# Value projection by rows, carried to the windows through DRAM, in a window-attention and mixture-of-experts kernel

## The chip, the cores and the metric

The kernel runs on one core of a Trainium2 chip. A core has a matmul engine (TensorE, "PE" in the profile, its weight loads "PEld"), VectorE ("DVE"), ScalarE ("ACT"), GpSimd ("POOL") and SyncE ("SP"), which here only issues DMA transfers. The metric is the device time of one execution in microseconds (us), as the median of several runs; less is better.

## The reference

The input `x` is (2, 128, 256, 256) in float32. It goes through a normalisation over channels, a window attention with a residual, a second normalisation and a mixture of eight experts with a residual.

```
x = x + conv(ln_c(x))                 # window attention
t = tokens(x)
t = t + ffn(ln_t(t))                  # top 2 of 8 experts

conv: qkv = W_qkv · x;  queries from 8 x 8 windows,
      keys and values from 12 x 12 windows around them (padding 2, outside the image 0)
      attn = softmax(q·k * scale + relative position + fixed mask)
      out  = W_out · (attn · v)       # 4 heads of 32 channels
ffn:  p = softmax(t · router_w + b);  the two largest, made to sum to 1
      out = sum over the two of p_e * (t · expert_w[e] + expert_b[e])
```

The fixed mask leaves, of each 12 x 12 window, only every second row and column that has the parity of the query's own. So the image falls into four planes (row parity by column parity) that do not meet in the attention; in each, a window has 4 x 4 queries and 6 x 6 keys.

## The kernel before

The image is cut into strips of eight rows, 32 for each of the two images. A strip has four planes of 4 x 128 positions. The main loop (from L779) goes over all 256 planes; one iteration does the attention of plane n, the projections of plane n + 1 (`project`), the normalisation and routing of rows (`norms`, `route`), and the experts of a quarter of an earlier strip (`Experts`). The order of instructions on every engine in this loop is the order of the program text (`manual_schedule`), so an engine that waits holds up everything written after it.

Two windows side by side share their keys and values in a run of 10 columns by 6 rows, 60 positions in a slot of 64. A plane has 16 such pairs; two pairs at a time fill 128 partitions (`HP` is 8). `xn` holds the normalised input of a strip with channels in the partitions, by plane, row (six: one row above, four, one below, `KR`) and column. `place` says at which of the six places of a window a row stands; the places turn from strip to strip, so that four rows are new in a strip and two stay.

The values need the positions in the partitions. Before the change, `columns` (L326) lets POOL copy the windows' columns from `xn` into `xcol`, overlaps included. Then `project` multiplies each of the eight column blocks of 128 with the weights `wv` (`values`, L366): four products into a PSUM tile `pvv` at the start of the projections, four more at their end, each group copied to `vv` by ACT (L376). `attend` (L477) uses `vv` as the weights of its products (L496).

The other steps that the prediction speaks of, in their order within an iteration:

- TensorE: the scores of plane n (L448, then L465), values and `pu` (L384), `pk` (L396), `pq` (L418), four expert products (L686), the attention (sums L486, values L496), the row sums `plt` (L554), the other values, three expert products, `po` (L524), one expert product. A float32 product is two passes, each a weight load and a matmul.
- DVE: routing (L587 to L619), `gT` (L625), the transpose `uT` of `pu` (L386), `au` (L349, L354), `xs` (L671) and six products `xe` (L677), the end of the experts (L692), the transposes and the division of the attention (L506 to L516), `plg` (L563), `rstd` (L228 to L235, with ACT for the logarithm and the exponential in L232 and L233), the residual `xt` (L529).
- POOL: a marker copy `last` (L681) that holds POOL back until DVE has made its six products, the two other products `xe` (L677), `ln1` (L272) between them, the halo copy (L246) in every fourth plane, and the columns of plane n + 2 (L331).
- SP: two `gd` transfers (L633), `rb` (L637, a row that `ln1` waits for), `sb` (L666), eight `gb` (L661), a load `xt` (L115), a store (L722). Before a `gb` fetch, ACT or DVE touches the tile, which holds the transfer back until then.

PSUM tiles named by `mm_tile` share three buffers in rotation: a tile gets the buffer of the one three before it and waits until that one has been read.

From n = 6 on, `addr_align` (L793) fills TensorE's instructions up so that every iteration begins at the same slot of a block of 256, in which instructions are fetched; `FIRST_LIMIT` instructions of the iteration lie in its first block.

Of the kernel before, what the change touches and what calls it, by code (L numbers as in the profile page):

```python
# [17 lines left out]
P = 128  # L18
# [25 lines left out]
KR, KC = 6, 10  # L44
NK = KR * KC
SLOT = 64
BLOCK, FIRST_LIMIT = 256, 95
NU = 9


# [1 line left out]
def kernel(  # L52
# [42 lines left out]
    def ctile(shape, name):  # L95
        return const.tile(shape, F32, tag=name, name=name)
# [101 lines left out]
    xn, xcol, kcol = [], [], []  # L198
    for i in range(2):
        xn.append(ctile([P, 2, 2, KR, PC + 2], f"xn{i}"))  # L200
        nc.gpsimd.memset(xn[i][:, :, :, :, 0 : PC + 2 : PC + 1], 0.0)
    for i in range(4):
        xcol.append(ctile([P, HP, 2, SLOT], f"xcol{i}"))
        kcol.append(ctile([P, NP, SLOT], f"kcol{i}"))
        nc.gpsimd.memset(xcol[i][:, :, :, NK:], 0.0)
        nc.gpsimd.memset(kcol[i][:, :, NK:], 0.0)
        nc.gpsimd.memset(kcol[i][:, 0, 0:NK:KC], 0.0)
        nc.gpsimd.memset(kcol[i][:, NP - 1, KC - 1 : NK : KC], 0.0)
# [9 lines left out]
    def rstd(p4, k0, k1, name):  # L218

        u, r = (
            small.tile([P, 2, NT], F32, tag=v, name=f"{v}_{name}")[:, k0:k1] for v in ("u", "r")
        )
        mean, sq = (
            p4[:, :, E + 2 * k0 + j : E + 2 * k1 : 2].rearrange("p t k -> p k t") for j in range(2)
        )
        nc.vector.tensor_copy(r, mean)  # L228
        nc.vector.tensor_tensor(u, r, r, ALU.mult)
        nc.vector.scalar_tensor_tensor(u, u, -1.0, sq, ALU.mult, ALU.add)  # L230
        nc.vector.scalar_tensor_tensor(u, u, 0.0, epsc[:, k0:k1], ALU.max, ALU.add)
# [23 lines left out]
    def runs(i, rows):  # L255

        out = []
        for k in rows:
            if out and place(i, k) == out[-1][1] + out[-1][2]:
                out[-1][2] += 1  # L260
            else:
                out.append([k, place(i, k), 1])
        return out
# [59 lines left out]
            ln1(i, k, pb, nc.vector)  # L323
        yield

    def columns(n):  # L326

        i, pl = divmod(n, 4)
        for k, at, m in runs(i, ln_rows(i)):
            for half in range(2):  # L330
                nc.gpsimd.tensor_copy(  # L331
                    xcol[pl][:, :, half, at * KC : (at + m) * KC].rearrange(
                        "p t (r c) -> p t r c", c=KC
                    ),
                    windows(xn[i % 2][:, pl // 2, pl % 2, k : k + m], half * HP, HP),
                )
        for k, s in ((0, 0), (KR - 1, NS - 1)):
            if strips[i][1] == s:
                c0 = place(i, k) * KC
                nc.gpsimd.memset(xcol[pl][:, :, :, c0 : c0 + KC], 0.0)  # L340
                nc.gpsimd.memset(kcol[pl][:, :, c0 : c0 + KC], 0.0)

    def shift(uT, n, state):

# [12 lines left out]
    def project(n, state):  # L357

        i, pl = divmod(n, 4)
        xp = xn[i % 2][:, pl // 2, pl % 2]  # L360
        inner = xp[:, 1 : 1 + PR, 1 : PC + 1]
        xl, kk = xcol[pl], kcol[pl]

        vv = work.tile([P, HP, P], F32, tag="vv", name=f"vv{n}")

        def values(t0):  # L366
            pv = mm_tile(f"pvv{n}_{t0}")
            for t in range(4):
                nc.tensor.matmul(  # L369
                    pv[:, t * P : (t + 1) * P],  # L370
                    lhsT=xl[:, t0 + t].rearrange("p a k -> p (a k)"),
                    rhs=wv,
                    start=True,
                    stop=True,
                )
            nc.scalar.copy(vv[:, t0 : t0 + 4, :].rearrange("p t c -> p (t c)"), pv)  # L376

        values(0)
        yield

        pu = mm_tile(f"pu{n}")
        nc.tensor.matmul(pu, lhsT=wrel, rhs=inner, start=True, stop=True)  # L384
        uT = work.tile([P, PR, 4, 32], F32, tag="uT", name=f"uT{n}", bufs=1)
        nc.vector.transpose(uT, pu.rearrange("p (a m s) -> p a s m", a=PR, s=4))  # L386
# [28 lines left out]
        yield  # L415

        pq = mm_tile(f"pq{n}")
        nc.tensor.matmul(pq, lhsT=wq, rhs=inner, start=True, stop=True)  # L418
        qs = work.tile([P, 2 * NP, PR, 4], F32, tag="qs", name=f"qs{n}")
        nc.scalar.copy(  # L420
            qs.rearrange("p m a s -> p a m s"), pq.rearrange("p (a m s) -> p a m s", a=PR, s=4)
        )
        yield

        values(4)
        state.update(qs=qs, kk=kk, vv=vv)
        yield

    def windows(rows, n0, count):
# [315 lines left out]
            next(part)  # L745
    if len(strips) > 1:
        halo(1)
    columns(0)
    states = {0: {}}
    for _ in project(0, states[0]):  # L750
        pass
    states[0]["shift"]()
    if n_planes > 1:
        columns(1)

# [22 lines left out]
    with tc.manual_schedule(engines={ET.PE, ET.DVE, ET.Activation, ET.Pool, ET.SP}):  # L778
        for n in range(n_planes + 7):  # L779
# [32 lines left out]
            next(ahead, None)  # L812
            if n + 1 < n_planes:
                states[n + 1]["shift"]()
            next(ahead, None)
            next(ahead, None)
            for e in (4, 6, 7, 5):
# [26 lines left out]
            new.fetch(3, dve)  # L844
            while to_store:
                store(*to_store.pop())
            next(ahead, None)
            ex.product(0)
            made = next(norm, None)
# [76 lines left out]
```

The softmax here doesn't subtract the row's maximum and nothing guards it: scores larger than these inputs give would overflow.

## Time and profile before

| what | us |
| --- | --- |
| median of three runs | 4484.65 |
| lowest and highest run | 4484.2 and 4484.88 |
| span of the profiled execution, first to last instruction | 4480.1 |
| PE busy | 4422.6 |
| DVE busy | 3996.2 |
| ACT busy | 1467.7 |
| POOL busy | 1317.7 |

For the profiled execution the profile gives the span; the 4.55 us between it and the median of the runs are what lies around it. The mean granted clock of TensorE is 0.997. In the 40 equal slices of the span every engine's share is the same from the second slice to the last but one, so one plane of the loop stands for all. A line of the groups names the source line, engine, operation, output and inputs, shapes and count, then the busy time and the mean of one (ns), and after the bar the engine's idle time ahead of it with what ended that. A line of the timeline gives the start, the length, the engine, the line and the tiles. A line of the waits says who waited for whom, for how long in all, how often, and the longest. A line of the windows gives a stretch, its length and the busy time of each engine (PE, PEld, DVE, ACT, POOL) with the number of instructions, then the granted clock, the share of the DMA engines and GB/s.

### The profile page before, as it was taken

Reading aid. Unit: us, or ns where it says so; the run is one execution under the profiler, and the core shown is the slowest. Engines: PE = TensorE matmul, PEld = TensorE weight load, DVE = VectorE, ACT = ScalarE, POOL = GpSimd, SP = SyncE. Lnnn points to the kernel's source line nnn. Section 1 sums busy time; section 2 is a strip of 40 time slices with the busy share of each in tenths; the row PEclk is TensorE's granted clock in tenths of the full one; section 3 lists DMA queues with packets and bytes.
Section 4 is the critical chain, followed back from the end, with each engine's and each line's share of the span. In section 5 each row is a group of like instructions: output and inputs, shape, how many; then the busy total and the mean of one; then the engine's idle time right before and its main releaser. Section 6 shows DMA issues by size and latency. Waiting matters only on the chain. (4 is left out here: it accounts for less than half of the span.)

```text
span 4480.1 us, 224632 instructions
## 1 busy us (share of the span) xinstructions
PE 4422.6 (99%) x96321; PEld 2683.3 (60%) x96321; DVE 3996.2 (89%) x11850; ACT 1467.7 (33%) x4022; POOL 1317.7 (29%) x1815
## 2 busy tenths in 40 slices
PE   7999999999999999999999999999999999999997
PEld 5666666666666666666666666666666666666653
DVE  5899999999899999998989999999999999989887
ACT  3333333333333333333333333333333333333321
POOL 1232323232323233232323232323232323232321
PEclk9999999999999999999999999999999999999999
DMA  2565666566656666666666566666665666566655
GB/s 83 174 191 185 192 185 192 186 191 185 193 184 192 185 191 187 189 188 188 189 187 189 187 190 185 193 183 193 184 193 185 192 185 192 186 191 186 190 164 186
DMA packets 519284, 828.12 MB, mean 185 GB/s; under 512 B 124186, under 2 KB 125850, under 8 KB 518298
## 3 DMA queue, kind: packets, MB, share of 16 engines
q1 hardware_dynamic: 517568, 813.46, 58.3%
q8 instruction: 769, 12.60, 1.1%
q14 instruction: 217, 1.78, 0.2%
q10 hardware_dynamic: 730, 0.29, 0.0%
HBM read 737.95 MB, written 75.56 MB: 182 GB/s over the span
## 5 line engine op out<-in xcount | busy, mean ns | idle before, releaser
L686 PE MATMUL acc<-xe,ew 128*128 128x512 f32 x4096 | 1889.0, 594 | 19.6 <-DVE gb L660 18.8
L686 PEld LDWEIGHTS acc<-xe,ew 128*128 128x128 f32 x4096 | 758.8, 190 | 885.7 <-issue 861.8
L677 DVE TENSOR_TENSOR xe<-xs,gb 128x512 f32<-128x512 f32 x1536 | 950.9, 687 | 10.2 <-PE acc L686 0.7
L681 POOL COPY last<-xe 128x1 f32<-128x1 f32 x256 | 47.9, 187 | 3060.8 <-DVE gb L660 3054.6
L376 ACT COPY vv<-pvv 128x512 f32<-128x512 f32 x512 | 299.8, 586 | 1395.7 <-PE pvv L369 1379.6
L677 POOL TENSOR_TENSOR xe<-xs,gb 128x512 f32<-128x512 f32 x512 | 650.8, 1272 | 5.9 <-PE att L496 2.5
L369 PE MATMUL pvv<-wt,xcol 128*128 128x128 f32 x4096 | 594.3, 288 | 2.5 <-POOL xcol L331 1.5
L369 PEld LDWEIGHTS pvv<-wt,xcol 128*128 128x128 f32 x4096 | 496.4, 191 | 64.8 <-issue 51.8
L272 POOL TENSOR_TENSOR xn<-xt,rb 128x512 f32<-128x512 f32 x249 | 375.0, 1506 | 66.5 <-DMA rb<-gd 55.9
L465 PE MATMUL att<-qs,kcol 32*64 32x32 f32 x32768 | 392.4, 226 | 0.8 <-issue 0.7
L465 PEld LDWEIGHTS att<-qs,kcol 32*64 32x64 f32 x32768 | 391.0, 130 | 1.0 <-issue 1.0
L496 PEld LDWEIGHTS att<-pT,vv 64*32 64x32 f32 x32768 | 348.0, 105 | 39.4 <-issue 2.5
L496 PE MATMUL att<-pT,vv 64*32 64x32 f32 x32768 | 343.2, 200 | 2.3 <-issue 2.3
L473 ACT ACTIVATE pT<-att 128x1024 f32<-128x1024 f32 x256 | 261.9, 1023 | 243.1 <-PE att L465 239.7
L548 ACT ACTIVATE sq<-xt 128x512 f32<-128x512 f32 x505 | 292.7, 631 | 0.0
L354 DVE STREAM_TRANSPOSE au<-auT 128x512 f32<-128x512 f32 x256 | 269.2, 1052 | 9.0
L524 PE MATMUL po<-o,wt 128*128 128x512 f32 x512 | 262.0, 593 | 6.1 <-DVE o L516 3.2
L384 PE MATMUL pu<-xn,wrel 128*128 128x512 f32 x512 | 262.5, 594 | 0.0
L407 ACT COPY kcol<-pk 128x560 f32<-128x560 f32 (+2 forms) x344 | 174.1, 506 | 268.2 <-PE pk L396 265.3
L418 PE MATMUL pq<-xn,wt 128*128 128x512 f32 x512 | 262.0, 593 | 0.0
L396 PE MATMUL pk<-xn,wt 128*128 128x512 f32 (+2 forms) x528 | 261.0, 578 | 0.0
L386 DVE STREAM_TRANSPOSE uT<-pu 128x512 f32<-128x512 f32 x256 | 182.8, 714 | 78.0 <-PE pu L384 77.0
(2697 smaller groups left out, 5243.8 us busy)
## 6 DMA issues: line engine op xcount, KB each, us to landing
gb<-gd SPq DMA_DIRECT2D x2048, 256.0 KB, 4.0
xt<-in_x_dram SPq DMA_DIRECT2D x256, 256.0 KB, 4.9
sb<-gd SPq DMA_DIRECT2D x256, 256.0 KB, 3.5
out_dram<-xt SPq DMA_DIRECT2D x256, 256.0 KB, 4.2
rb<-gd SPq DMA_DIRECT2D x249, 256.0 KB, 3.3
gd<-gT SPq DMA_DIRECT2D x516, 16.0 KB, 3.0
ew<-in_L_ffn_expert_w_dram SPq DMA_DIRECT2D x1, 512.0 KB, 5.0
eb<-in_L_ffn_expert_b_dram SPq DMA_DIRECT2D x1, 512.0 KB, 5.7
```

What stands on the lines that cost most here:

```text
L272: eng.tensor_tensor(xn[i % 2][:, :, :, k, 1 : PC + 1], ln1_src(i, k).rearrange("p (y j x) -> p y x j", y=2, x=2), rb.rearrange("p (y j x) ...
L354: nc.vector.transpose(au.rearrange("p m a s -> p a s m"), auT[n % 2])
L369: nc.tensor.matmul(pv[:, t * P : (t + 1) * P], lhsT=xl[:, t0 + t].rearrange("p a k -> p (a k)"), rhs=wv, start=True, stop=True,)
L376: nc.scalar.copy(vv[:, t0 : t0 + 4, :].rearrange("p t c -> p (t c)"), pv)
L384: nc.tensor.matmul(pu, lhsT=wrel, rhs=inner, start=True, stop=True)
L418: nc.tensor.matmul(pq, lhsT=wq, rhs=inner, start=True, stop=True)
L465: nc.tensor.matmul(sc[rows, h, 32 * t : 32 * t + 32], lhsT=kk[hp, half * HP + t, :], rhs=qs[hp, m0 : m0 + 2].rearrange("p m a s -> p (m a ...
L496: nc.tensor.matmul(av[hp, half, 32 * t : 32 * t + 32], lhsT=vv[rows, t, hp], rhs=pT[rows, h, 32 * t : 32 * t + 32], start=True, stop=True,)
L524: nc.tensor.matmul(po, lhsT=wo, rhs=state["o"].rearrange("p f z -> p (f z)"), start=True, stop=True)
L548: nc.scalar.activation(sq, src, AF.Square)
L677: eng.tensor_tensor(self.xe[e], self.xs, self.gb.pop(e), ALU.mult)
L686: nc.tensor.matmul(self.acc, lhsT=ew[:, e, :], rhs=self.xe.pop(e), start=(e == 0), stop=not self.xe)
```

## The change

`columns` and `xcol` go. Each row of a strip's plane that is new is projected once: its 128 positions are the columns of one product with `wv`, four rows into one PSUM tile `pv` (five rows in an image's first strip, three in its last), and ACT copies the tile to `vr` (`value_rows`). `pu` stands ahead of these products. SP writes `vr` into a DRAM tile `vrows` by place and position (`send_values`, after the `uT` and `au` steps), and later in the same iteration, after the store, reads it back into the windows `vwin` (`take_values`): one transfer for each new row and each half of the pairs, over ten partitions with eight pieces of 512 bytes. `vwin` has the layout that `vv` had, and keeps the two rows that stay. The border columns of `vrows` are zeroed once; `borders` zeroes the rows outside the image.

In `rstd`, the square of the mean takes one factor from PSUM (`mean`) and no longer both from the copy `r`. `FIRST_LIMIT` goes from 95 to 99.

```diff
-BLOCK, FIRST_LIMIT = 256, 95
+BLOCK, FIRST_LIMIT = 256, 99
...
+    zero = ctile([P, 2, P], "zero")
+    nc.gpsimd.memset(zero, 0.0)
...
-        xcol.append(ctile([P, HP, 2, SLOT], f"xcol{i}"))
+        vwin.append(ctile([P, HP, P], f"vwin{i}"))
-        nc.gpsimd.memset(xcol[i][:, :, :, NK:], 0.0)
+        vrows.append(dram.tile([KR, PC + 2, P], F32, tag=f"vrows{i}", name=f"vrows{i}", bufs=1))
+        nc.gpsimd.memset(vwin[i], 0.0)
+        nc.sync.dma_start(vrows[i][:, 0 : PC + 2 : PC + 1, :], zero[0:KR])
...
-        nc.vector.tensor_tensor(u, r, r, ALU.mult)
+        nc.vector.tensor_tensor(u, r, mean, ALU.mult)
...
+    def value_rows(n):
+        i, pl = divmod(n, 4)
+        xp = xn[i % 2][:, pl // 2, pl % 2]
+        rows, sent = list(ln_rows(i)), []
+        for part in (rows[-4:], rows[:-4]):
+            if not part:
+                continue
+            pv = mm_tile(f"pv{n}_{part[0]}")
+            m = len(part)
+            for j, k in enumerate(part):
+                nc.tensor.matmul(pv[:, j * P : (j + 1) * P],
+                    lhsT=xp[:, k, 1 : PC + 1], rhs=wv, start=True, stop=True)
+            vr = work.tile([P, 4, P], F32, tag="vr", name=f"vr{n}_{part[0]}")
+            nc.scalar.copy(vr[:, 0:m].rearrange("p r c -> p (r c)"), pv[:, : m * P])
+            sent.append((part, vr))
+        return sent
+    def send_values(n, sent):
+        i, pl = divmod(n, 4)
+        for part, vr in sent:
+            for k, at, m in runs(i, part):
+                nc.sync.dma_start(
+                    vrows[pl][at : at + m, 1 : PC + 1, :].rearrange("r c d -> c r d"),
+                    vr[:, k - part[0] : k - part[0] + m])
+    def take_values(n):
+        i, pl = divmod(n, 4)
+        s = strips[i][1]
+        for k in range(0 if s == 0 else 2, KR):
+            at = place(i, k)
+            for half in range(2):
+                p0 = half * SLOT + at * KC
+                src = vrows[pl][at, half * HP * 8 : half * HP * 8 + KC, :].unsqueeze(1)
+                dims = [list(d) for d in src.ap]
+                dims[1] = [8 * P, HP]
+                nc.sync.dma_start(vwin[pl][p0 : p0 + KC],
+                                  bass.AP(src.tensor, src.offset, dims))
...
-        values(0)
-        yield
         pu = mm_tile(f"pu{n}")
         nc.tensor.matmul(pu, lhsT=wrel, rhs=inner, start=True, stop=True)
+        state["sent"] = value_rows(n)
+        yield
...
-        values(4)
-        state.update(qs=qs, kk=kk, vv=vv)
+        state.update(qs=qs, kk=kk, vv=vwin[pl])
...
                 states[n + 1]["shift"]()
+                send_values(n + 1, states[n + 1]["sent"])
...
                 store(*to_store.pop())
+            if n + 1 < n_planes:
+                take_values(n + 1)
...
-                columns(n + 2)
+                borders(n + 2)
```

More of the change, by code (lines that the diff above doesn't have):

```diff
@@ L196 @@
     nc.vector.tensor_copy(wrel, pr[:, :P])
-    xn, xcol, kcol = [], [], []
+    xn, vwin, vrows, kcol = [], [], [], []
+    zero = ctile([P, 2, P], "zero")
+    nc.gpsimd.memset(zero, 0.0)
     for i in range(2):
@@ L324, in first_norms, with borders @@
         yield
-    def columns(n):
+    def borders(n):
         i, pl = divmod(n, 4)
[L329 to L336, printed above, removed]
         for k, s in ((0, 0), (KR - 1, NS - 1)):
@@ L338, in columns @@
             if strips[i][1] == s:
-                c0 = place(i, k) * KC
-                nc.gpsimd.memset(xcol[pl][:, :, :, c0 : c0 + KC], 0.0)
-                nc.gpsimd.memset(kcol[pl][:, :, c0 : c0 + KC], 0.0)
+                at = place(i, k)
+                nc.gpsimd.memset(kcol[pl][:, :, at * KC : (at + 1) * KC], 0.0)
+                nc.sync.dma_start(vrows[pl][at, 1 : PC + 1, :], zero[:, 0, :])
+    def value_rows(n):
[8 more added lines that the diff above has]
+            for j, k in enumerate(part):
+                nc.tensor.matmul(
+                    pv[:, j * P : (j + 1) * P],
+                    lhsT=xp[:, k, 1 : PC + 1],
+                    rhs=wv,
+                    start=True,
+                    stop=True,
+                )
+            vr = work.tile([P, 4, P], F32, tag="vr", name=f"vr{n}_{part[0]}")
+            nc.scalar.copy(
+                vr[:, 0:m].rearrange("p r c -> p (r c)"), pv[:, : m * P]
+            )
+            sent.append((part, vr))
+        return sent
@@ new lines, in send_values @@
+    def send_values(n, sent):
[4 more added lines that the diff above has]
+                    vrows[pl][at : at + m, 1 : PC + 1, :].rearrange("r c d -> c r d"),
+                    vr[:, k - part[0] : k - part[0] + m],
+                )
+    def take_values(n):
+        i, pl = divmod(n, 4)
+        s = strips[i][1]
+        for k in range(0 if s == 0 else 2, KR):
+            at = place(i, k)
+            for half in range(2):
[3 more added lines that the diff above has]
+                dims[1] = [8 * P, HP]
+                nc.sync.dma_start(
+                    vwin[pl][p0 : p0 + KC], bass.AP(src.tensor, src.offset, dims)
+                )
@@ L361, in project @@
         inner = xp[:, 1 : 1 + PR, 1 : PC + 1]
[L362 to L376, printed above, removed]
-        values(0)
-        yield
+        kk = kcol[pl]
         pu = mm_tile(f"pu{n}")
         nc.tensor.matmul(pu, lhsT=wrel, rhs=inner, start=True, stop=True)
+        state["sent"] = value_rows(n)
+        yield
         uT = work.tile([P, PR, 4, 32], F32, tag="uT", name=f"uT{n}", bufs=1)
@@ L747 @@
         halo(1)
-    columns(0)
+    borders(0)
     states = {0: {}}
@@ L752 @@
     states[0]["shift"]()
+    send_values(0, states[0]["sent"])
+    take_values(0)
     if n_planes > 1:
-        columns(1)
+        borders(1)
     onesm = ctile([P, P], "onesm")
```

## The prediction

> **What bounds the kernel now.** I read the page first, for the busy shares, then the stretch of one plane.
>
> ```profile
> span 4480.1 us, 224632 instructions
> PE 4422.6 (99%) x96321; PEld 2683.3 (60%) x96321; DVE 3996.2 (89%) x11850; ACT 1467.7 (33%) x4022; POOL 1317.7 (29%) x1815
> ...
> 2001.45:2018.61 17.16, 17.16 (x377) 10.42 (x377) 15.80 (x49) 5.87 (x17) 5.20 (x8) 1.00 0.62 192
> ```
>
> The third line is the window from one plane's first L448 matmul to the next one's: PE is busy in all 17.16 us, DVE in 15.80, at clock 1.00. The starts of all planes from 20 to 239, tallied from the trace, repeat every 17.165 us with hardly a deviation: TensorE sets the pace. DVE has little room, though. The groups and the waits come next:
>
> ```profile
> L369 PE MATMUL pvv<-wt,xcol 128*128 128x128 f32 x4096 | 594.3, 288 | 2.5 <-POOL xcol L331 1.5 <-issue 1.0
> L331 POOL COPY xcol<-xn 128x160 f32<-128x160 f32 (+3 forms) x672 | 237.6, 391 | 0.1
> DVE uT L386 <- PE pu L384: 77.0, 186, 7.9
> ```
>
> The value products are 16 records a plane (two passes for each of eight). The 77 us are nearly all that DVE waits for TensorE, 0.3 us a plane. Then the timeline of the same plane, PE, DVE and POOL:
>
> ```profile
> 2005.45 0.72 DVE L386 STREAM_TRANSPOSE uT<-pu 128x512 f32<-128x512 f32 x1
> 2006.11 1.02 PE L418 MATMUL pq<-xn,wt 128*128 128x512 f32 x2
> ...
> 2013.23 1.16 PE L369 MATMUL pvv<-wt,xcol 128*128 128x128 f32 x8
> ...
> 2014.93 1.27 POOL L677 TENSOR_TENSOR xe<-xs,gb 128x512 f32<-128x512 f32 x1
> 2015.39 0.83 DVE L229 TENSOR_TENSOR u__116_37779<-r__116_37780 128x8 f32<-128x8 f32 x1
> 2016.26 0.16 DVE L230 SCALAR_TENSOR_TENSOR u__116_37779<-u__116_37779,plg 128x8 f32<-128x8 f32 x1
> 2016.45 0.29 DVE L231 SCALAR_TENSOR_TENSOR u__116_37779<-u__116_37779,epsc 128x8 f32<-128x8 f32 x1
> 2016.80 1.02 PE L524 MATMUL po<-o,wt 128*128 128x512 f32 x2
> 2017.86 0.69 DVE L529 TENSOR_TENSOR xt<-po,xt 128x512 f32<-128x512 f32 x1
> ```
>
> L229 works on 8 elements a partition and takes 0.83 us; it ends at 2016.22, when POOL's L677 ends (2016.20). In the ten planes where no POOL operation runs beside it, it takes 0.163 us. L230, with one operand in PSUM, takes 0.16 beside POOL's copies. So a DVE operation with both inputs in SBUF can wait for POOL's running operation, and 0.67 us of this one is such a wait. Last, the DMA queue:
>
> ```profile
> SPq L637 <- DMA gd<-gT: 457.2, 249, 3.2
> rb<-gd SPq DMA_DIRECT2D x249, 256.0 KB, 3.3
> gd<-gT SPq DMA_DIRECT2D x516, 16.0 KB, 3.0
> ```
>
> SP issues in order, 14 transfers a plane, with the semaphores of only eight transfers: each issue first waits for the one eight before it.
>
> **TensorE.** Eight value products become four (five in a first strip). The late group goes: its first matmul starts at 2013.23 and the next operation's at 2014.22, less 0.11 for that one's own weight load, so 0.88 us. `pu` and the four remaining products change places at equal cost. TensorE alone would need 17.165 − 0.88 = 16.28 us. Added: the first attention product must wait for up to eight transfers; a separate semaphore instruction on PE takes 51 ns, and I count three or four, against the few instructions queued ahead of it: 0 to 0.2 us, taken as 0.1, because single ones leave no gap in the trace.
>
> **The block limit.** A plane is 768 slots now (752 matmul instructions, 2 semaphore instructions, 14 padding NOPs). Sixteen matmul instructions go and a few waits come, so about 26 NOPs, 71 ns apart. They are dispatched after `o` is ready (13.46 us into the plane), and until the next L448 there are 3 us of matmuls: 1.9 us fit. Without that cover, 12 more NOPs would cost 0.85 us a plane. The limit itself, 95 to 99: the block still ends inside L465, whose PE idle time is 0.8 us in the whole run; I take nothing. From below there is nothing to win; from above, the unaligned first plane shows one 1.0 us stall of issue, which would be 250 us in all.
>
> **DVE.** Times from here are means over planes 20 to 239, counted from the plane's first L448 matmul. In three planes of four, L229 starts at 13.94, POOL's L677 ends at 14.76 and L231 ends at 15.21. With `mean` in PSUM, L229 takes 0.16 like L230, L230 follows, and L231 could start at 14.33; but L231 has `u` and `epsc`, both in SBUF. Its own record is mixed: median 168 ns, coming 0.31 us into one of POOL's copies, but 286 ns in 87 planes, where it comes in a copy's first 0.07 us and ends 20 ns after it. If it always passes, it ends at 14.49; if it waits for L677, at 14.77. I take the wait, because L229 beside this same L677 nearly always pays it: gain 15.21 − 14.77 = 0.44. The Trainium skill, "SBUF — State Buffer", section "SBUF: two separate sides", has it that an operation with two SBUF inputs and a GpSimd operation exclude each other for the whole instruction; by that rule it is 14.77, by L231's median 14.49.
>
> Two more waits shrink once TensorE is ahead: DVE's before L386, 0.27 us (`gT` is done at 3.73, uT starts at 4.00), because `pu` comes 0.88 us earlier; and L529's for `po`, 0.10 us. What is late next is DVE itself: 17.165 − 0.44 − 0.27 − 0.10 = 16.35 us. In the fourth plane, where POOL also copies the halo (0.62 us), L677 ends at 15.20; there DVE has neither of the two small waits, so only 0.44 goes: 16.72. Mean over four: 16.44. That is above TensorE's 16.28 to 16.48: DVE becomes the bound by a little.
>
> **A new wait.** Of three rotating `mm` buffers, the order of before gave `pq` the buffer of the first values; with seven tiles a plane (pu, pv, pk, pq, plt, plg, po) it gets that of `pu`. So `pq` must wait for L386, and behind it on TensorE stand four expert products and the whole attention, for which DVE's L506 waits. L386 ends 0.72 after its start; semaphore and weight load bring `pq` to 0.91, where before it was 0.66: attention 0.25 us later, plus the 0.1 above. L231's wait for POOL leaves 14.77 − 14.49 = 0.28 of cover in ordinary planes and more in the fourth. From 0 to 0.35 us; I take 0.05.
>
> **SP and the transfers.** Added: one or two sends and eight takes a plane (twelve in a first strip). Issue times in the rows are 0.32 to 0.59 us, so ten take about 4 us; SP's instructions fill about 5.5 of 17. After the store (14.4) the takes need until about 18.5, because the last wait for the xt load and the store; then four `gb` fetches, wanted by DVE or POOL 7 us later. The values are wanted 25.8 after the plane's start and land at 21 to 22. One chain is tight: on ACT the copy of `pv` stands ahead of the `gb` copy whose fetch stands ahead of `gd` on SP. It comes about 1.0 us later (`pu` first, TensorE later), so `gd` is issued at 5.3 for 4.26 and `rb` lands at 11.6 for 10.53; POOL's L272 wants it at 12.02. 0 to 0.4 us, taken as 0.04, because only the slowest landings reach that far.
>
> The engines: packets of 512 B took 27 ns (1,536 weight packets). 512 to send and 640 to take are 1,152 × 27 ns / 16 = 1.9 us more on 10.6 (0.62 of 17.16): 76% busy at the new pace. The Trainium skill, "DMA: Bandwidth & Descriptors", section "Why a DMA increments its semaphore by 16 and not by 1", says a transfer over ten partitions uses ten engines. By it, ten engines get 2.6 us more and stand at 80%; that speaks against the takes, and changes nothing in the sum.
>
> POOL loses its copies L331 (0.9 us a plane), ACT one copy of 0.59; neither sets the end.
>
> **The sum.** 16.44 + 0.05 + 0.04 = 16.53 us a plane, 0.635 less, over 249 planes: 158 us. Once: a bigger pad at the first aligned plane (104 NOPs there now, about 170 then, 71 ns each: +5); the first attention waiting for values through DRAM (+4); the early planes lose three products each (−3). Span 4480.1 − 158 + 6 = 4328; the runs' median lies 4.55 above the profiled span, so 4333 us.
>
> **The rivals.** *TensorE still sets the pace* (12%): L231 passes, the halo planes average out: 16.28 a plane, 4484.65 − 249 × 0.885 + 6 = 4270. For it: L231's median; against it: L229.
>
> *The wait only moves* (13%): L231 takes over L229's whole wait in time, or the `pq` wait lies bare with 0.35: 16.85 to 16.88, so about 4412 to 4420. For it: DVE is 89% busy.
>
> *Slower: eight transfers in flight* (8%). With 24 transfers a plane, three rounds of eight must land: 3 × the mean landing time. At 3.0 to 4.9 us (rows) that is 12 us, below the pace; from 5.72 us it is the plane, and at 6.0 us 18.0, so 4484.65 + 249 × 0.835 = 4693. For it: DMA engines are already 80 to 90% busy from 12 to 16 us of the plane, where the takes come; against it: they are idle right after.
>
> *Nothing changes* (2%): landing times near 5.7.
>
> **How the numbers follow.** The main case has 65%, its own range 4290 to 4380. Eight in ten: from the TensorE bound, 4270, to just beyond the moved wait, 4425. A measurement of this kernel tells about 0.2%, 9 us. Faster 0.88, same 0.03, slower 0.09.
>
> **What would show it.** Right: 2,048 value matmul records for 4,096; L229 at 0.16 us and L231 ending with POOL's L677; a PE wait at `pq` for L386; a plane of 16.4 to 16.6 us with one longer in four. Wrong: L231 at 0.17 beside L677, PE without idle time, SP waiting at the takes, or `rb` as the releaser of L272.

## The result, and the profile after

The changed kernel takes 5165.52 us (median of four runs, 5144.18 to 5275.03) against 4484.42 us (four runs, 4482.26 to 4484.88): a ratio of 1.1505, 95% interval 1.1482 to 1.1529; the ratio leaves out the run of 5275.03 us, which counts as slow. The profiled execution is the one of 5144.18 us. Means over planes are again over planes 20 to 239, tallied from the trace; a plane now begins with L477.

First the page, then the windows of two planes that follow each other:

```profile
span 5142.3 us, 226264 instructions
PE 4526.1 (88%) x94273; PEld 2583.0 (50%) x94273; DVE 4045.4 (79%) x11850; ACT 1308.9 (25%) x3774; POOL 1093.9 (21%) x1128
```

```profile
2139.64:2161.47 21.83, 17.86 (x369) 10.44 (x368) 14.73 (x47) 5.05 (x14) 4.12 (x4) 0.92 0.60 181
2161.47:2177.74 16.27, 16.27 (x369) 9.53 (x368) 14.61 (x45) 5.05 (x14) 4.15 (x4) 1.00 0.66 193
```

The second plane is the one that was predicted for TensorE alone: 16.27 us, no idle time, full clock. The first does the same work in 21.83. Planes mix the two: 70 of the 220 take 16.27, each of them alone between longer ones; the median is 20.29, the mean 19.78. The groups and the waits answer to those of before:

```profile
L350 PE MATMUL pv<-wt,xn 128*128 128x128 f32 x2048 | 273.0, 276 | 0.2 <-DVE gb L689 0.2
L715 PE MATMUL acc<-xe,ew 128*128 128x512 f32 x4096 | 2096.7, 649 | 20.8 <-DVE gb L689 18.5
L525 PE MATMUL att<-pT,vwin 64*32 64x32 f32 x32768 | 370.7, 202 | 377.2 <-issue 377.2
```

```profile
POOL xn L276 <- DMA rb<-gd: 592.7, 219, 26.1
PE att L525 <- issue: 377.2, 130, 5.5
...
PE pq L448 <- DVE uT L416: 153.7, 112, 2.2
...
DVE uT L416 <- PE pu L411: 33.3, 14, 11.8
```

The waits of the kernel before had, for the first two:

```profile
POOL xn L272 <- DMA rb<-gd: 55.9, 4, 24.7
PE att L496 <- issue: 2.3, 2, 1.3
```

The value products are 2,048 records instead of 4,096, as told. New are three things: the row update on POOL waits for `rb` 219 times (4 before); the attention values stand 377 us on "issue", that is, in no wait for a semaphore that the profile shows; and `pq` waits 154 us for `uT`, where before it had no such wait. The timeline of the slow plane shows the second, first TensorE, then the windows of the stretch before the stall, the stall and the stretch behind it:

```profile
2149.14 1.20 PE L525 MATMUL att<-pT,vwin 64*32 64x32 f32 x105
2154.31 0.44 PE L525 MATMUL att<-pT,vwin 64*32 64x32 f32 x23 [3.97 <-issue]
```

```profile
2146.40:2150.34 3.94, 3.94 (x127) 2.14 (x126) 3.89 (x10) 0.67 (x3) 0.54 (x2) 1.00 0.41 111
2150.34:2154.31 3.97, 0.00 (x1) 0.00 (x0) 0.00 (x0) 0.00 (x0) 2.75 (x3) 0.97 0.83 213
2154.31:2158.30 3.99, 3.99 (x58) 2.56 (x58) 2.83 (x8) 0.00 (x0) 0.83 (x1) 0.61 0.64 230
```

After 105 of the 128 matmuls TensorE stops for 3.97 us with DVE and ACT idle too, and then runs on a clock of 0.61. The tally finds this stall in 109 of 220 planes ahead of the same record, number 105 when counted from 0, with a median of 2.75 us; nothing in the data is special there. Counted in instructions, the record lies where a block of 256 ends (slot 99 + 512). The trace has the queue that brings the blocks (16 KB, 0.95 us each, three a plane): in each of the 109 TensorE goes on 1.2 to 1.6 us after such a transfer has ended, and the transfer began between 0.6 us before and 2.6 us after TensorE's stop, in the median 0.2 after. It came when the instructions had run out. In the kernel before, the transfers came a block ahead: the one for this boundary had ended at least 2.1 us before TensorE got there in 99 planes of 100, and the one for the next boundary began 0.8 to 3.5 us after this one. The trace shows when a transfer begins, not when it was asked for; by a late block, or a late request, I mean below a block whose transfer began only when TensorE had all but run out of instructions (0.6 us ahead of its stop or later).

Where the 19.78 − 16.28 = 3.50 us a plane go: stalls at L525 326 us, at `pq` 138, elsewhere 17, which is 2.2 us a plane; and 543 us at half clock, 2.47 a plane, of which half is lost, 1.2. The sum is 3.4.

SP is the other new place. Its timeline in the same plane, and its waits over the run:

```profile
2135.21 6.79 SPq L385 DMA_DIRECT2D vwin<-vrows  x8
2142.10 2.56 SPq L690 DMA_DIRECT2D gb<-gd  x4
2144.77 1.40 SPq L662 DMA_DIRECT2D gd<-gT  x2
2148.49 0.33 SPq L666 DMA_DIRECT2D rb<-gd  x1
```

```profile
SPq L666 <- DMA gd<-gT: 734.6, 249, 4.6
SPq L385 <- DMA gb<-gd: 622.9, 904, 2.8
```

The eight takes hold SP for 6.79 us here, 6.4 on the mean: most of them stand until the transfer eight before them has landed and go out 0.02 us later, one every 0.7 us in the median. So the `gb` fetches and `gd` behind them are late, and `rb`, which in this kernel is issued 11.8 us into the plane on the mean, is late too; it was issued at 7.4 before. Of the eight takes of a plane, 5.8 go out only after the plane that reads them has begun.

### The profile page after: what moved, and what is told of

The parts are those of the page before. It is cut to its first block, busy times and chain, and to the rows that moved or that the text cites. A ratio compares the mean times of both kernels' runs of the same rounds, so it can differ in the third digit from the quotient of the medians.

```text
span 5142.3 us, 226264 instructions
## 1 busy us (share of the span) xinstructions
PE 4526.1 (88%) x94273; PEld 2583.0 (50%) x94273; DVE 4045.4 (79%) x11850; ACT 1308.9 (25%) x3774; POOL 1093.9 (21%) x1128
## 3 DMA queue, kind: packets, MB, share of 16 engines
q14 instruction: 229, 1.88, 0.1%
## 5 line engine op out<-in xcount | busy, mean ns | idle before, releaser
L715 PE MATMUL acc<-xe,ew 128*128 128x512 f32 x4096 | 2096.7, 649 | 20.8 <-DVE gb L689 18.5
L715 PEld LDWEIGHTS acc<-xe,ew 128*128 128x128 f32 x4096 | 832.2, 209 | 1067.4 <-issue 998.2
L706 DVE TENSOR_TENSOR xe<-xs,gb 128x512 f32<-128x512 f32 x1536 | 962.4, 687 | 103.1 <-DMA gb<-gd 89.6
L525 PE MATMUL att<-pT,vwin 64*32 64x32 f32 x32768 | 370.7, 202 | 377.2 <-issue 377.2
L706 POOL TENSOR_TENSOR xe<-xs,gb 128x512 f32<-128x512 f32 x512 | 649.6, 1270 | 1.9 <-DMA gb<-gd 1.0
L525 PEld LDWEIGHTS att<-pT,vwin 64*32 64x32 f32 x32768 | 358.9, 106 | 429.4 <-issue 390.5
L535 DVE STREAM_TRANSPOSE sT<-att 128x512 f32<-128x512 f32 x256 | 183.5, 717 | 430.8 <-PE att L525 428.7
L350 PEld LDWEIGHTS pv<-wt,xn 128*128 128x128 f32 x2048 | 271.2, 193 | 128.5 <-issue 67.6
L558 DVE TENSOR_TENSOR xt<-po,xt 128x512 f32<-128x512 f32 x256 | 176.1, 688 | 155.0 <-PE po L553 154.8
L411 PE MATMUL pu<-xn,wrel 128*128 128x512 f32 x512 | 293.4, 655 | 0.0
L350 PE MATMUL pv<-wt,xn 128*128 128x128 f32 x2048 | 273.0, 276 | 0.2 <-DVE gb L689 0.2
L621 ACT ACTIVATE lg<-lg 128x32 f32<-128x32 f32 x256 | 58.7, 229 | 835.6 <-DVE lg L620 835.6
```

The costliest lines, as they stand in the source:

```text
L350: nc.tensor.matmul(pv[:, j * P : (j + 1) * P], lhsT=xp[:, k, 1 : PC + 1], rhs=wv, start=True, stop=True,)
L525: nc.tensor.matmul(av[hp, half, 32 * t : 32 * t + 32], lhsT=vv[rows, t, hp], rhs=pT[rows, h, 32 * t : 32 * t + 32], start=True, stop=True,)
L706: eng.tensor_tensor(self.xe[e], self.xs, self.gb.pop(e), ALU.mult)
L715: nc.tensor.matmul(self.acc, lhsT=ew[:, e, :], rhs=self.xe.pop(e), start=(e == 0), stop=not self.xe)
```

## The experiments

All but the timed one are single runs beside the kernel before (4482 to 4488 us). The changed kernel's own four runs differ by 2.5%, so differences below that between two variants above 5000 us are not read.

**The number of transfers, their packets, and who issues them.** `no_takes` leaves the takes out of the loop (the windows keep what they had ahead of it); `thin_takes` reads one of a take's eight pieces, into one eighth of its place; `double_takes` splits each take in two; `takes_on_act` lets ACT issue them.

```diff
-                take_values(n + 1)                       # no_takes
-                dims[1] = [8 * P, HP]                    # thin_takes
+                dims[1] = [8 * P, 1]
-                nc.sync.dma_start(vwin...                # takes_on_act
+                nc.scalar.dma_start(vwin...
```

> The changed kernel without the takes inside the loop (the windows' values stay what the prologue left; the sends stay). Theory SP: the eight takes hold SP's in-order queue (8.1 us of its 19.8 a plane), so the gate rows and the values come late; without them a plane is TensorE's 16.3 to 16.5 us and the time 4260 to 4340 us. Rival packets: the 512-byte packets load the DMA engines; 512 of 1,152 stay, so the time falls about halfway, to 4600 to 4800. Rival TensorE: pq's wait for uT and the half clock after it set the loop, whatever is transferred; over 4900.

> As many takes as in the changed kernel, but each brings one of its eight blocks (10 packets for 80); the other blocks stay what they were. Theory SP: an issue and a wait each as before, so 4900 to 5150 us. Rival packets: seven eighths of the takes' packets are gone, 4300 to 4500.

> Each take split into two over four blocks each: the same packets, twice the transfers. Theory SP: eight more issues at 0.65 us each on SP, a plane of about 24 to 25 us, 6100 to 6500 us. Rival packets: the same packets, 5100 to 5250.

> The takes issued by ACT in place of SP, at the same place of the program text; the same packets and the same eight semaphores. Theory SP as a matter of SP's order: SP loses its 8.1 us, a plane of 16.3 to 17 us, 4270 to 4450 us. Theory SP as a matter of the eight semaphores alone: the transfers behind the takes still wait for them, 4800 to 5150. Rival packets: 5100 to 5200.

Measured: 4425.04, 5093.83, 5950.61 and 5189.90 us. So the takes are the loss, and by their number: an eighth of the packets changes little, twice the transfers for the same bytes cost nearly 800 us more. As sizes, two of my figures missed: `no_takes` lies 85 us above its range and `double_takes` 150 below. The 5189.90 us fall into the range that I had given to the packets, which `thin_takes` rules out; on ACT the wait only changes place, as ACT's timeline shows:

```profile
2143.35 9.97 ACTq L385 DMA_DIRECT2D vwin<-vrows  x8
2153.36 0.21 ACT L236 ACTIVATE r__107_34988<-u__107_34987 128x8 f32<-128x8 f32 x1 [14.49 <-DMA vwin<-vrows]
```

ACT stands 10 us in the takes, and the statistics of the next rows behind them. In this kernel the attention values have no stall at the block boundary at all.

**Two takes instead of eight, and the order of the gate fetch.** `two_takes` orders a window's 60 positions by column, then row, and `vrows` likewise, so that one transfer over 60 partitions fills a half. `two_takes_fetch7` and `no_takes_fetch7` also issue the gate fetch 7 behind `gd` and `rb`, so that ACT's copy does not hold these up.

```diff
-        for k in range(0 if s == 0 else 2, KR):
-            at = place(i, k)
-            for half in range(2):
+        for half in range(2):
...
+            dims[1] = [8 * KR * P, HP]
```

> The 60 positions of a window turned from row by column to column by row, in DRAM, keys and values alike: a plane's values come in two takes of 480 packets for eight of 80, half as many packets again in a quarter of the transfers; the sends become packets of up to 2 KB. Theory of the count (each take costs SP an issue and a wait for one of eight semaphores, 0.4 to 1 us, whatever it holds): six fewer, a plane falls from 19.8 to about 17, 4400 to 4520 us, near the kernel without takes (4425). Rival packets: more of them, 5150 us or more.

> The same, and the touch for the gate row of expert 7 on ACT goes ahead of the copy of the row products, so that its fetch, and with it the two gd transfers and rb behind it on SP, leave about 1 us earlier. Theory: that 1 us is what holds POOL's L272 (ln1) back; 16.4 to 16.7 us a plane, 4300 to 4390 us. Rival (the gates are late because transfers are slow, not because they leave late): as two_takes.

> The changed kernel without the takes inside the loop (as in no_takes, the windows' values stay what the prologue left), and the touch for expert 7 first on ACT. Theory that gd leaves late: the plane falls from 16.86 us to 16.3 to 16.55, 4280 to 4345 us. Rival (TensorE's wait for uT and POOL's lock keep it at 16.86): 4410 to 4430.

Measured: 4675.66, 4658.94 and 4407.23 us. All three miss the ranges of my theory. Without takes but with the late fetch, the row update's wait for `rb` falls from 175.1 us (139 times) to 49.0 (6 times), yet the time by only 18 us: the late `gd` does delay `rb`, as I had it, but little hangs on that alone. With two takes that wait is 502 us, and the whole still 190 us above the kernel before.

**The mean's factor alone**, in the kernel before:

```diff
-        nc.vector.tensor_tensor(u, r, r, ALU.mult)
+        nc.vector.tensor_tensor(u, r, mean, ALU.mult)
```

> The kernel before with one edit: the square of the mean takes a factor from PSUM. TensorE sets the pace there, so 4475 to 4490 us, no change; in the profile L229 falls to 0.16 us, and L231 ends with POOL's operation beside it (theory of the lock) or stays at 0.17 us (rival: one small operation slips through).

Measured: 4481.99 beside 4486.02 us, nothing where TensorE is the bound. The trace settles the other question. L229 takes 0.16 us, and L231 now ends with POOL's operation:

```profile
2001.53 1.27 POOL L677 TENSOR_TENSOR xe<-xs,gb 128x512 f32<-128x512 f32 x1
2001.62 1.19 DVE L231 SCALAR_TENSOR_TENSOR u__115_37452<-u__115_37452,epsc 128x8 f32<-128x8 f32 x1
```

So it does in 217 of 220 planes, with a median of 0.44 us where it had 0.17 before the edit. In three planes of four it ends 14.78 us into the plane on the mean.

**The place of the block boundary.** `limit_95` and `limit_107` set `FIRST_LIMIT`, nothing else.

> The changed kernel with its instruction-block limit back at 95, nothing else. Block theory: TensorE stands because its next block of 256 instructions has not come. In the changed kernel the stall in the attention values always sits ahead of their record 105, and in 109 of 220 planes the transfer of that block begins only after TensorE has reached the boundary; 103 of these 109 are planes in which the transfer of the block before began less than 2.6 us ahead of the q product. Then the stall moves with the limit, four slots or two matmuls back, to record 103 (in the scores from record 17 to 15), and the boundary between them lies two expert matmuls (0.8 us) earlier, so that a transfer has to begin 3.4 us ahead of the q product instead of 2.6 us: 200 or more of 220 planes miss it, and with 22.6 us for such a plane and 17.1 us for another the mean is 21.5 to 22.5 us: 5500 to 5750 us. Rival, the transfers alone decide and the place of the boundary does not matter: records 105 and 17 as before, 5110 to 5200 us.

> The changed kernel with the limit at 107 instead of 99. Block theory: stall at record 109 of the attention values; the boundary ahead of it is four expert matmuls (1.65 us) later, so the block before it may begin as late as 0.9 us ahead of the q product, which only some 8 of 220 planes exceed: the on-demand stalls nearly vanish. The next block is then asked for 1.65 us later, which leaves short stalls of 0.5 us a plane on the mean, and with them most of the half clock goes: 17.3 to 18.0 us a plane, 4540 to 4720 us. Rival, transfers alone: 5110 to 5200 us.

Measured: 5244.19 and 5241.84 us. The timelines of TensorE, `limit_95` first:

```profile
2019.92 1.12 PE L525 MATMUL att<-pT,vwin 64*32 64x32 f32 x103
2026.00 0.45 PE L525 MATMUL att<-pT,vwin 64*32 64x32 f32 x25 [4.96 <-issue]
```

```profile
2030.87 1.17 PE L525 MATMUL att<-pT,vwin 64*32 64x32 f32 x109
2034.77 0.31 PE L525 MATMUL att<-pT,vwin 64*32 64x32 f32 x19 [2.73 <-issue]
```

Four slots less move the stall two matmuls back, eight more move it four on: it is the block boundary. The times were a miss in both directions. I had a stall decided by where the boundary ahead of it lies; but 122 and 136 planes stalled against 109, and both times lie within the spread of the changed kernel. With the limit at 107 most of the blocks that came too late (116 of 136) were still those whose predecessor began less than 2.6 us ahead of `pq`, as with 99 (103 of 109). So the limit of 99 is worth nothing that could be read, and why the request fails stays open.

**The waits in TensorE's stream.** In the changed kernel TensorE has four instructions at the head of L525 that only wait for the takes' semaphores:

```profile
L525 PEldq EVENT_SEMAPHORE  x1024: 51/51/216, 38.2 to 5055.6; - x171
```

The kernels with two takes or none have none there, and showed 0 to 3 planes with a late request, although the blocks ahead of it came no earlier. I count the time from the start of the preceding transfer to the boundary that it serves. In the changed kernel all 79 planes with less than 4.5 us led to a late request; `no_takes` has 187 such planes and none did, `two_takes` 196 and two did. `takes_on_act` is the reverse case: three such waits, no plane with less than 5.2 us, and no stall. `waits_early` moves them behind `pq`:

```diff
-BLOCK, FIRST_LIMIT = 256, 99
+BLOCK, FIRST_LIMIT = 256, 105
...
+            if n < n_planes:
+                cols = vwin[pl][:, 0, 0:32]
+                nc.tensor.matmul(states[n]["att"][0:32, 2, HQ : HQ + 32],
+                    lhsT=cols, rhs=cols, start=True, stop=True)
             for e in (4, 6, 7, 5):
```

> The changed kernel with one added 32 x 32 matmul that reads a strip of the window tile just after the q product, so that TensorE's four waiting instructions for the eight takes stand there and no longer at the head of the attention values; the limit is 105, so that the boundary behind the q product stays at the fourth expert matmul. Theory that the four waits between the two boundaries keep the next block from being asked for (kernels without them, such as the one with two takes, showed 0 or 1 such plane in 220 with later transfers than here): on-demand stalls in under 20 planes, 4550 to 4750 us. Rival, the waits have nothing to do with it and the late block does it alone: 100 or more planes with on-demand stalls and 5080 to 5200 us.

Measured: 5037.99 us. TensorE's waits:

```profile
PE pq L448 <- DVE uT L416: 182.8, 181, 2.1
PE att L851 <- DMA vwin<-vrows: 122.1, 115, 2.8
...
PE att L525 <- issue: 28.0, 66, 1.7
```

The stall at L525 falls from 377 to 28 us, and no plane has a late request, although some 125 of 220 preceding blocks began as late (less than 2.4 us ahead of `pq`) as those that led to one in the changed kernel. Counted to the boundary, before which TensorE now waits, only 17 began under 4.5 us ahead. By either count the late block alone is not enough, so the waits behind it are part of the condition; that they act by themselves, and not through something else that the takes bring, is argued. But the time moves by less than the spread, and missed my range: TensorE now waits for the takes themselves (L851 is the added product) and for `uT`. With the stall gone the plane still takes 19.37 us, so there is a second cause.

**SP's queue.** `two_takes_pool` gives the two takes (with fetch 7 late) to POOL; `gates_on_pool` gives `gd` and `rb` to POOL and leaves the eight takes on SP; `two_takes_gates_pool` does that with two takes.

```diff
-                nc.sync.dma_start(to[k], gT[:, k])
+                nc.gpsimd.dma_start(to[k], gT[:, k])
...
-            nc.sync.dma_start(rb, to_all(gd, E + 1))
+            nc.gpsimd.dma_start(rb, to_all(gd, E + 1))
```

> The kernel with two takes a plane and the gate fetch 7 issued after the spread (4659 us), with its two takes issued by GpSimd, which has semaphores of its own. Theory that SyncE's order with its eight semaphores delays gates and rows: SyncE no longer waits for takes nor counts them, and the time falls towards that of the kernel without takes (4407 us): 4420 to 4540 us. Rival, the bytes and packets on the shared DMA engines make the landings long: within 1 per cent of 4659 us. Against it: GpSimd's issue may take its own time and come after the product with the gates, so that the values land late: above 4700 us.

> The changed kernel with the two gd stores and the rb load issued by GpSimd instead of SyncE; everything else, the eight takes included, as it is. Theory that SyncE's queue is the bound: in the changed kernel SyncE spends 10.8 us a plane issuing and 6.5 us (1652 us in 256 planes) waiting for transfers, 17.2 us against TensorE's 16.28 us. Without the waits for gd to land (735 us, 2.9 us a plane) and the issue of gd and rb (about 1.2 us) its need falls to 13 us, below TensorE: 16.7 to 18.0 us a plane, 4400 to 4720 us, and the row update on GpSimd no longer waits 593 us for rb. Rival, the eight takes' packets and completions fill the DMA engines whoever issues the rest: gd and rb land as late as before, 5050 to 5200 us. Second rival, GpSimd's own issue of three transfers (0.74 us each where it issued the takes) pushes the row update onto VectorE's statistics as it did there: 4800 to 5050 us.

> The kernel with two takes a plane (4675.66 us) with gd and rb issued by GpSimd. SyncE theory: rb lands early again, the row update is off VectorE's statistics (their two-operand lines went from 102 to 327 us with two takes), the q product no longer waits for uT (171 us with fetch 7 behind the spread): 4400 to 4500 us, level with or ahead of the kernel before. Rival, the landing times under the added bytes decide: 4600 to 4680 us.

Measured: 5038.71, 5284.48 and 4471.72 us. The first is the case "against it": POOL stands in the takes until the sends have landed, and its work comes late and in one piece, here with the DVE line that it holds up:

```profile
2005.05 1.48 POOL L382 DMA_DIRECT2D vwin<-vrows  x2 [13.59 <-DMA vrows<-vr]
...
2006.67 1.27 POOL L703 TENSOR_TENSOR xe<-xs,gb 128x512 f32<-128x512 f32 x1
2007.89 1.49 POOL L277 TENSOR_TENSOR xn<-xt,rb 128x512 f32<-128x512 f32 x1
2009.35 1.26 POOL L703 TENSOR_TENSOR xe<-xs,gb 128x512 f32<-128x512 f32 x1
```

```profile
2007.42 3.21 DVE L236 SCALAR_TENSOR_TENSOR u__102_32721<-u__102_32721,epsc 128x8 f32<-128x8 f32 x1
```

DVE's line on eight elements ends at 2010.63, with the last of POOL's three operations (2010.61). This line takes 673 us over the run, and 57 in `no_takes_fetch7`.

`gates_on_pool` missed: SP was freed (it waits 2136 us for compute engines, against 765), yet the time did not fall. The stall at the block boundary was left, 455 us in planes 20 to 239 for 326 in the changed kernel and 392 and 437 with the other limits:

```profile
PE att L525 <- issue: 540.8, 152, 5.8
```

**Both causes away.** `waits_early_gates_pool` has both edits, with the eight takes in place.

> Both edits at once: the takes' four waits moved behind the q product (alone 5038 us: almost no stall at a block boundary left, but SyncE's queue full) and gd and rb issued by GpSimd (alone 5284 us: SyncE has 8 us of slack a plane, but 455 us of stall at the block boundary). Theory of two causes, each of which alone is enough to keep a plane near 20 us: with both gone, block stalls under 40 us, few waits for the takes, 16.8 to 17.8 us a plane, 4430 to 4680 us. Rival, a third cause that both left in place (eight small transfers a plane on the DMA engines): 4950 to 5200 us.

Measured: 4594.88 us, as the theory of two causes says. TensorE's waits:

```profile
PE pq L448 <- DVE uT L416: 65.5, 115, 1.9
PE att L525 <- issue: 51.5, 91, 1.9
```

The four together, with their neighbours (SP's issue time a plane; SP's waits for transfers and for compute engines over the run, summed from its waits; the stall in the attention values and the half clock, planes 20 to 239; all in us):

| kernel | time | a plane | SP issues | SP waits, transfers | SP waits, compute | stall L525 | half clock |
| --- | --- | --- | --- | --- | --- | --- | --- |
| before | 4484 | 17.17 | 5.5 | 522 | 2608 | 0 | 0 |
| changed | 5144 | 19.78 | 10.8 | 1652 | 765 | 326 | 543 |
| `waits_early` | 5038 | 19.37 | 10.2 | 1813 | 635 | 20 | 249 |
| `gates_on_pool` | 5284 | 20.23 | 7.9 | 1025 | 2136 | 455 | 638 |
| `waits_early_gates_pool` | 4595 | 17.58 | 8.0 | 1298 | 1214 | 41 | 14 |
| `two_takes` | 4676 | 17.87 | 8.7 | 1617 | 1012 | 45 | 48 |
| `two_takes_gates_pool` | 4472 | 16.99 | 6.5 | 749 | 2081 | 21 | 10 |
| `no_takes` | 4425 | 16.87 | 7.4 | 660 | 1953 | 0 | 17 |

With either cause taken away alone, a plane stays near 20 us; with both, it falls by 2.2 us. The pair of kernels with two takes, neither of which has much stall at the boundary, shows the second cause by itself: the gates on POOL are worth 204 us there. In the changed kernel SP's issue and its waits for transfers, 10.8 + 1652 / 256 = 17.2 us a plane, are more than TensorE's 16.28; that SP is the bound by this sum is a reading, as the waits depend on the rest of the plane. The shortest planes of `waits_early_gates_pool` take 16.64 for 16.27, which I put down to the added product and its waits.

**Is there a version that beats both?** `two_takes_gates_pool` was timed in 12 runs, and its edit on the gates tried alone on the kernel before.

> The version with two takes and the gates on GpSimd once more, timed against the kernel before: 4471.7 us in one run beside 4488.4 us, so a ratio of 0.996, between 0.994 and 0.998. If the one run was by chance: 0.998 to 1.004.

> The kernel before with gd and rb issued by GpSimd, as a control for the version with two takes. There TensorE is busy in all of a plane's 17.165 us and rb lands in time, so the theory says that the issuing engine has no part in it: 4475 to 4495 us. If GpSimd's three issues push its products or the row update onto VectorE's statistics: 4500 to 4600 us. If the gain of the version with two takes came from this edit and not from the four fewer value products: below 4475 us.

Measured: 4472.61 us (median of 12 runs, 4437.43 to 4492.43) against 4485.96 (17 runs), ratio 0.9955, 95% interval 0.9934 to 0.9976. The gates alone: 4486.99 beside 4482.33 us, no gain. So the projection by rows does win, 0.45%, when two transfers carry it and the gates have a queue of their own.

## Why the prediction was wrong

**TensorE alone** (right): 16.28 was told, undisturbed planes take 16.27.

**DVE as the bound, 16.44 a plane** (not shown). The undisturbed planes stand singly, behind planes in which DVE could catch up, so they do not test it. The sum was too low without the takes as well: `no_takes` needs 16.87 us a plane and `no_takes_fetch7` 16.75, for the 16.53 that I had with them.

**The mean's factor** (right in its parts): L233 takes 0.16 us, and L235 takes over the wait for POOL, as I took it. In `mean_alone` the same operation, L231 there, ends at 14.78 for the 14.77 that I had. In the plane from 2161.47 of the changed kernel, the timelines of DVE and POOL have:

```profile
2175.42 0.16 DVE L233 TENSOR_TENSOR u__109_35634<-r__109_35635,plg 128x8 f32<-128x8 f32 x1
2175.61 0.16 DVE L234 SCALAR_TENSOR_TENSOR u__109_35634<-u__109_35634,plg 128x8 f32<-128x8 f32 x1
2175.81 0.72 DVE L235 SCALAR_TENSOR_TENSOR u__109_35634<-u__109_35634,epsc 128x8 f32<-128x8 f32 x1
2175.25 1.27 POOL L706 TENSOR_TENSOR xe<-xs,gb 128x512 f32<-128x512 f32 x1
```

L235 ends at 2176.53, POOL's L706 at 2176.52. The same operation's own median before, 168 ns, pointed the other way; the wait of its neighbour L229 told it.

**SP and the transfers** (the step that failed first). "Issue times in the rows are 0.32 to 0.59 us, so ten take about 4 us", done by 18.5. I used the issue time without the wait for the transfer eight before, although I had written that wait down, and landings from a kernel with 14 transfers. Measured: the eight takes alone hold SP for 6.4 us on the mean, start 18.4 us after the plane's start and end at 24.8. Landings lengthened, of `gb` to about 5.5 us from 4.0, of the xt load to 7.3 from 4.9, of the store to 6.8 from 4.1 (medians); but they are as long in `no_takes` (5.9, 7.4 and 6.3 us), so it is not the takes that lengthen them, and by themselves they did not cost the time. Behind the takes `rb` landed 14.7 us into the plane in the median, not at 11.6, and POOL's row update met DVE's statistics: of these, L235 takes 135 us over the run for the 57 of `no_takes_fetch7`, L238 144 for 45. In `two_takes_gates_pool`, where `rb` goes out at 8.6 us again, the wait of `pq` for `uT` falls from 191 us in `two_takes` to 39 (planes 20 to 239), as it must if this is what made `uT` late.

**The wait of `pq`** (mechanism right, size off): taken at 0.05 us a plane, with 0.35 as its upper end; 138 us in 220 planes are 0.63, because DVE was late for the reason above.

**The block limit** (the other step that failed). I costed the place of the boundary and the padding (27 NOPs for my 26, and hidden as told), took nothing, and named 1.0 us a plane, 250 us, as the upper end. I did not ask when the transfer of a block begins, nor what moves it. It came to 326 us of stall, and the half clock behind it, which I had in no term. The four waiting instructions on TensorE I had counted (three or four) and priced at 0.1 us by their 51 ns; their place cost far more than their length.

**The DMA engines** "76% busy, changes nothing" (right): `thin_takes` shows that packets are not the cost. The takes' transfers are. That a take uses ten engines fits the trace: it leaves 11 updates of its semaphore, where a transfer over 128 partitions leaves 16.

**The rival of eight transfers in flight** had the right sign and the right queue, not the mechanism. Its price was three times the mean landing time; that is 3 × 4.6 = 13.8 us here, below the pace, and would have decided nothing. SP does not keep eight in flight: it stands in order, at the takes, then at `gd`, and adds these waits to its issue time. And its 4693 us had no second cause in it.

The Trainium skill has a rule for the failed block step. "Runtime: NRT & Kernel Launch", section "Instruction fetch mechanics", says that an engine fetches the next 16 KiB of instructions through a DMA queue of its own while it executes, and that the cost of a boundary is mostly hidden. The kernel before agrees, with no stall in 220 planes; the changed one does not, with 109 stalls of 2.75 us in the median. The measurement decides: in these runs the boundary is hidden where the transfer begins a block ahead, and not where it begins when TensorE has run out.

Left open: why a separate wait in TensorE's stream, together with a late block, goes with a next block that comes only on demand. The runs show the condition from three sides (moved waits, no waits, waits without a late block), not its mechanism. That the mean's factor costs nothing in the changed kernel itself was not tried.

## What to carry to other kernels

Price an added DMA at its queue, not at its bytes: issue time, plus the wait for the transfer that holds its semaphore, plus what stands behind it in order; and sum issue and waits of that queue against the pace. Where "issue" idle time always sits ahead of the same matmul record, count instructions to see whether a block ends there, compare with the transfers on the queue of the blocks, and look for the engine's separate wait instructions ahead of it. When taking one cause away does not move the time, take two away at once before dropping either.

## What the hardware showed that I had not expected

- An idle TensorE loses its clock sooner than I thought. In the changed kernel (planes 20 to 239), of 125 stalls of 2.0 us or more 121 were followed by half clock, of 67 under 1.5 us none; over the run it lasts 3.4 us (111 times) or 6.8 (40 times). What counts there is idle time within a window: half clock begins only at points of a grid of 3.413 us that runs through the whole trace. Of 1,116 windows of this grid at full clock, all 105 with more than 1.88 us idle were followed by half clock, and none of the 971 with less than 1.59. At half clock, a window with 0.39 us idle or more was followed by another one (33 times), one with 0.35 or less by full clock. The Trainium skill, "TensorE: Matmul & The Clock Gate", section "What's actually happening", has half clock after an idle window of about 3.4 us. The lengths agree with that window; idle time of about half of it was enough.
- After a late block, TensorE went on 1.2 to 1.6 us after the end of its transfer. In planes without that stall, the transfer for the next boundary began up to 5.9 us after the boundary in the attention values in the changed kernel, 3.5 in the one before (99 planes of 100).
- A DVE operation with both inputs in SBUF can wait through three POOL operations in a row (3.21 us above, up to 5.1 us in that run), not only through the one that runs when it comes.
